# A graph-network layer with 203 instead of 191 of its 391 edge blocks summed by sorting on the chip

## The chip, the cores and the metric

One core of one Trainium2 chip runs the program. The metric is the time of one execution in microseconds on the device, the median over runs. Engines are named as in the profile: PE (TensorE matmul) with PEld (its weight loads), DVE (VectorE), ACT (ScalarE), POOL (GpSimd) and SP (SyncE, which here only issues DMAs).

## The reference

200,000 edges join 6,250 nodes, with 128 features a node. The edges come sorted by `dst`; `src` is random.

```python
h = jnp.maximum(_layernorm(x, axis=-1), 0.0)
x_ = h @ W_in
W_ij = shifted_softplus(f_ij @ W_f1 + b_f1) @ W_f2 + b_f2      # f_ij: 20 features an edge
W_ij = W_ij * f_ij_cutoff
x_ij = x_[dst] * W_ij                                           # one row of 128 an edge
out = jax.ops.segment_sum(x_ij, src, num_segments=6250)         # summed by source node
return x + shifted_softplus(out @ W_o1 + b_o1) @ W_o2 + b_o2
```

## The kernel before

**Items and quads.** The edges are cut into 1563 chunks of 128, and four chunks make a *quad* (512 edges); there are 391. The main loop runs over *items*, one for each quad, and is unrolled in full: item i carries the stages of several quads, each at its own distance. For every quad PE computes `z` (L374), ACT the softplus in two steps (L379, L384), PE the filter `W` (L567, eight float32 passes) and the gather of node rows `xg` by a one-hot matmul (L559), ACT the scaled copy `xc` (L572), and DVE the product of `W` and `xc` (L582). What differs is how the rows of a quad reach their source nodes.

**Scattered quads.** 200 of the 391 write their product into a tile `s` (six buffers). POOL then issues one indirect DMA with accumulation for each chunk (L644, four for a quad), which adds 128 rows of 128 floats into one of four accumulators in DRAM, `acc0` to `acc3`. The first 12 of these quads ("plain") are first cleaned of rows with the same node by a matmul (`pp`, L594); the other 188 ("listed", in windows of 16 quads) find such rows by the comparison `eql` (L427) and the counts `lcnt` (L437), and each window ends with one scatter more. Which accumulator a scatter uses follows from its number: `acc_of` goes round two up to K2_END, three up to K3_END, then four, and leaves out `acc0` for the last 64. `acc2` and `acc3` are zeroed by SP's DMAs at the items in Z2 and Z3, ten pieces of 320 KB each.

**Grouped quads.** The other 191 (quads 8, 10, 12 ... 388; `mpq`, from MP0, MPGAPS and MPEND in `sorted_quads`) never go to DRAM. DVE splits the product in three bf16 parts (`part_rem`, L746, twice a quad) and makes one-hot columns `pm` (L732, four). PE permutes the rows by node group (`pq`, L758, eight matmuls) and takes out those that find no slot (`po`, L781, four), ACT copies the results (`sg`, L766, four), SP regroups them by four DMAs (`mst`, L773). Eight such quads make a *round*, which has four *units*: in a unit PE multiplies the regrouped rows with one-hot rows `so` (made by DVE, L845) in 12 matmuls a quad of 32 rows each (`un`, L860), and DVE adds the four results into `accT` in SBUF (L871). Rows without a slot are summed once for two quads (`over_pe` to `over_int`) and go to DRAM in one scatter.

**Order.** It is written out by hand: `put` and `at` hang each step on an item and on a point in it (`L`, `D0`, `PE1`, `PE2`, `D2` and so on; table `AT`), and each engine runs its own instructions strictly in the order in which they were recorded, apart from what the weight loads do ahead. `unit_slots` places the units on items of grouped quads whose third last was not grouped.

**The end.** After scatter 843 no scatter goes to `acc0`. From item 372 on, `acc0` is read back group by group (`r0t`, L1171), transposed by PE (`rtp`, L1178) and added to `accT` (L1184), beside the last items. After the last scatter and the last unit the tail reads `acc1` to `acc3` (L1513) and computes the output layer.

Of the kernel before, what the change touches and what calls it, by code (L numbers as in the profile page):

```python
# [8 lines left out]
BF16 = mybir.dt.bfloat16  # L9
I32 = mybir.dt.int32  # L10
# [10 lines left out]
P = 128  # L21
# [5 lines left out]
OVC = 128  # L27
SLOTS = GRP * BCAP + OVC
MP0 = 8
MPGAPS = (2,)  # L30
MPEND = 1
RND = 8
RKQ = 8
ULAG = 7
# [21 lines left out]
LLAG = 12  # L56
LASTLAG = 5
LCAP = 7
LZERO = (9, 11, 13, 45)
PW = 387  # L60
MW = 388
PREP_GAP = 9
# [13 lines left out]
def tile_gnn(ctx: ExitStack, tc: tile.TileContext, x, fB, cT, srcT, srcr, srci, dstr, win_, wf1, wf2, bias, bo1c, wo1,  # L76
# [20 lines left out]
    GN = NP // GRP  # L97
    ZR = 10 if ACC_R % 10 == 0 else 1
    ZEARLY = 3
    K1_END, K2_END, K3_END = 0, 16, 170  # L100
    Z2, Z3 = [0, 1, 1, 2, 2, 3, 3, 4, 4, 5], range(18, 58, 4)
    mpq = sorted_quads(NQ)
    mpi = {q: n for n, q in enumerate(mpq)}
    rounds = unit_rounds(mpq)
    uslots = unit_slots(rounds)
    units = {i for us in uslots for i in us}
# [31 lines left out]
    wk = edge.enter_context(tc.tile_pool(name="wk", bufs=2))  # L138
# [669 lines left out]
        mp[q]["row"] = t  # L808

    def over_eq(q):  # L810
        eq = wk.tile([P, P], BF16, tag="oeq", name="oeq", bufs=1)
        nc.vector.tensor_scalar(eq, mp[q].pop("row")[:, :P], mp[q]["so"], None, op0=ALU.is_equal)
        mp[q]["eq"] = eq

# [104 lines left out]
    with tc.manual_schedule():  # L919
# [126 lines left out]
        def at(i, point, fn, *a):  # L1046
            hooks.setdefault((i, point), []).append((fn, a))

        def put(name, base, fn, *a, busy=()):
            d, point = AT[name]  # L1050
            i = max(clear(base + d, busy) if busy else base + d, 0)
            at(i, point, fn, *a)
            return i
# [66 lines left out]
        busy = units | {prep_start(g) + k for g in range(1, NG) for k in range(5)}  # L1120
# [85 lines left out]
        if spread:  # L1206
            k = clear(mid + 9, busy, 2)
# [3 lines left out]
            k = clear(NQ - 1, busy, 2)  # L1211
# [25 lines left out]
        for r in range(-(-len(mpq) // RKQ)):  # L1237
# [5 lines left out]
            k = put("rk_count", i, rank_count, r, busy=units)  # L1243
            k = max(k + 1, i + AT["rk_own"][0])
            at(k, AT["rk_own"][1], rank_own, r)
            k = clear(max(k, i + AT["rk_over"][0]), units)
            at(k, AT["rk_over"][1], rank_over, r)
            k = max(k + 1, i + AT["rk_slot"][0])
# [5 lines left out]
        for w in range(NW):  # L1254
            for g in range(wsize[w] // 4):
# [9 lines left out]
                k = put("l_dup", i, l_dup, w, g)  # L1265
# [12 lines left out]
            k = clear(i + AT["l_sum"][0], units)  # L1278
# [4 lines left out]
            k = put("l_int", k, over_int, ("L", w))  # L1283
            at(k, "S", over_scatter, ("L", w))
        if LE:
            for k in range(NACC):
                at(LZERO[k], "L", zero_list, k)
        for q in mpq:
            put("pm", q, perm_oh, q)
            put("rem1", q, part_rem, q, 1)  # L1290
            put("rem2", q, part_rem, q, 2)
            put("ext", q, part_ext, q)
            if q + 4 in units:
                for s in range(4):
                    at(q + 3, "PE2", permute, q, s)
                for s in range(4):
                    at(q + 3, "PE2", perm_out, q, s)
                for h in range(2):
                    at(q + 4, "L", regroup, q, h)
            else:  # L1300
                for s in range(4):
                    put(f"p{s}", q, permute, q, s)
                    put(f"o{s}", q, perm_out, q, s)
                for h in range(2):
                    put(f"rg{h}", q, regroup, q, h)
            if mpi[q] % 2 or q == mpq[-1]:
                k = mpq[mpi[q] + 1] if mpi[q] + 1 < len(mpq) else q + 2
                put("over_pe", k, over_pe, q)
                put("over_out", k, over_out, q)
                put("over_idx", q, over_idx, q)  # L1310
                put("over_dg", q, over_dg, q)
                k = put("over_row", q, over_row, q, busy=units)
                put("over_eq", k, over_eq, q)
                k = put("over_sum", q, over_sum, q, busy=units)
                put("over_copy", k, over_copy, q)
                put("over_ji", k, over_ji, q)
                k = put("over_int", k, over_int, q)
                at(k, "S", over_scatter, q)
        last = mpq[-1]
        for r, us in enumerate(uslots):  # L1320
            for s, k in enumerate(us):
                for h in range(3):
                    d, point = AT[f"so{h}"]
                    at(max(k + d, us[s - 1] if s else uslots[r - 1][3] if r else 0), point, unit_oh, r, s, h)
                put("unit", k, unit_pe, r, s)
                put("evac", k, unit_evac, r, s)

# [100 lines left out]
    with tc.For_i(0, redo, 1):  # L1428
# [8 lines left out]
        with tc.For_i(0, trips, 1) as ci:  # L1437
# [12 lines left out]
                cm, engines=[SP], min_val=0, max_val=EP // P - 1,  # L1450
                skip_runtime_bounds_check_because="a column of the table")
            nc.sync.dma_start(xcol, dropd[:, bass.ds(cr, 1)])
            sb = wk.tile([P, P], I32, bufs=1, tag="oeq", name="fsb")
            nc.sync.dma_start(sb, srcr.rearrange("s e -> (s e)")[bass.ds(ci * P, P)].unsqueeze(0).to_broadcast([P, P]))
            ft = wk.tile([P, P], BF16, tag="oh", name="fft")
            nc.vector.memset(ft[96:P, :], 1.0)
# [32 lines left out]
            eq = wk.tile([P, P], F32, tag="eq", name="feq", bufs=3)  # L1489
# [3 lines left out]
            s = wk.tile([P, P], F32, bufs=1, tag="dg", name="fs")  # L1493
# [118 lines left out]
def sorted_quads(nq):  # L1612
    qs, q = [], MP0
    while q < nq - MPEND:
        qs.append(q)
        q += MPGAPS[(len(qs) - 1) % len(MPGAPS)]
    return qs
# [10 lines left out]
def unit_slots(rounds):  # L1628
    end = rounds[-1][-1]
    grouped = {q for qs in rounds for q in qs}  # L1630
    out, used = [], set()
    for r, qs in enumerate(rounds):
        a = qs[-1] + ULAG
        last = r == len(rounds) - 1
        step = 2 if last else (rounds[r + 1][-1] - qs[-1]) / 4
        us = []
        for s in range(4):
            i = a + int(s * step)
            while i in used or (not last and i <= end and not UCLASSES[UCLASS](i, grouped)):
                i += 1  # L1640
            used.add(i)
            us.append(i)
        out.append(us)
    return out
# [10 lines left out]
def clear(i, busy, n=1):  # L1655
    while any(i + k in busy for k in range(n)):
        i += 1
    return i
# [11 lines left out]
def prep_start(g):  # L1670
    busy = unit_its(sorted_quads(4 * PREP_GAP * (g + 8)))
    return clear(7 + PREP_GAP * (g - 1), busy, 2) - 1
# [100 lines left out]
```

## Time and profile before

| | |
|---|---|
| median of 3 runs | 1912.47 us (1911.3 to 1914.54) |
| the profiled execution | 1918.46 us, of which the span of instructions 1916.7 us |
| mean granted TensorE clock | 0.96 |
| DMA engines' mean busy share | 0.8 in most slices of the span, 177 GB/s |
| scatters (L644) | 907: 751 of listed quads, 48 of plain ones, 108 of overflows and window sums |

The span divides into a start (to about 60 us), the loop over the items (to about 1825 us), the drain of the last grouped quads (to 1867 us) and the tail (to 1917 us). The profile's chain of what ended last reaches back only to 1867 us, and so covers the tail alone; what sets the pace of the loop must be read from the share of busy time of the engines in single stretches, and from who waits for whom.

### The profile page before, as it was taken

Reading aid. Unit: us, or ns where it says so; the run is one execution under the profiler, and the core shown is the slowest. Engines: PE = TensorE matmul, PEld = TensorE weight load, DVE = VectorE, ACT = ScalarE, POOL = GpSimd, SP = SyncE. Lnnn points to the kernel's source line nnn. Section 1 sums busy time; section 2 is a strip of 40 time slices with the busy share of each in tenths; the row PEclk is TensorE's granted clock in tenths of the full one; section 3 lists DMA queues with packets and bytes.
Section 4 is the critical chain, followed back from the end, with each engine's and each line's share of the span. In section 5 each row is a group of like instructions: output and inputs, shape, how many; then the busy total and the mean of one; then the engine's idle time right before and its main releaser. Section 6 shows DMA issues by size and latency. Waiting matters only on the chain. (4 is left out here: it accounts for less than half of the span.)

```text
span 1916.7 us, 55067 instructions
## 1 busy us (share of the span) xinstructions
PE 1676.3 (87%) x19124; PEld 1142.4 (60%) x19124; DVE 1600.0 (83%) x4692; ACT 1449.6 (76%) x4045; POOL 1509.3 (79%) x960
## 2 busy tenths in 40 slices
PE   4678898989998989989989989999999999978976
PEld 3555566656666666665656656666666566655644
DVE  5768897988898899899889888898897897976657
ACT  4668777867887888887878878887887888866615
POOL 5577768778888888888888888888888888887755
PEclk8789999999999999999999999999999999998988
DMA  8888888878888888888888888888888888868757
GB/s 294 229 197 198 191 186 173 175 153 160 172 180 168 162 177 172 162 188 162 164 175 180 168 171 178 174 179 174 173 183 155 172 183 170 169 121 185 130 116 267
DMA packets 366238, 339.58 MB, mean 177 GB/s; under 512 B 86685, under 2 KB 329292, under 8 KB 365956
## 3 DMA queue, kind: packets, MB, share of 16 engines
q1 hardware_dynamic: 233189, 269.78, 49.5%
q0 software_dynamic: 132208, 66.05, 33.0%
q8 instruction: 151, 2.47, 0.5%
q14 instruction: 132, 1.07, 0.2%
q10 hardware_dynamic: 558, 0.20, 0.0%
HBM read 151.16 MB, written 108.80 MB: 136 GB/s over the span
## 5 line engine op out<-in xcount | busy, mean ns | idle before, releaser
L644 POOL DMA_INDIRECT acc<-s,lji x751 | 1210.0, 1611 | 269.4 <-issue 177.0
L572 ACT ACTIVATE xc<-xg,cb 128x128 f32<-128x128 f32 x1564 | 447.5, 374 | 179.7 <-PE z L374 92.5
L567 PEld LDWEIGHTS W<-w,a 128*128 128x128 f32 x3128 | 430.0, 199 | 64.2 <-issue 50.9
L860 PE MATMUL un<-so,mst 32*128 32x392 bf16 x9168 | 425.1, 329 | 18.1 <-ACT sg L766 7.9
L567 PE MATMUL W<-w,a 128*128 128x128 f32 x3128 | 430.7, 282 | 0.8 <-issue 0.5
L766 ACT CAST sg<-pq 128x388 bf16<-128x388 f32 x764 | 342.1, 497 | 75.0 <-DMA mst<-sg 48.5
L758 PE MATMUL pq<-pt,pm 128*128 128x388 bf16 x1528 | 328.5, 337 | 30.5 <-ACT os L825 9.6
L860 PEld LDWEIGHTS <-mst 32*128 32x128 bf16 x9168 | 251.5, 94 | 166.8 <-issue 37.6
L384 ACT ACTIVATE a<-a,con 128x512 f32<-128x512 f32 x391 | 282.8, 723 | 11.6
L746 DVE TENSOR_TENSOR pt<-pt 128x512 f32<-128x512 f32 x382 | 259.6, 680 | 0.0
L871 DVE TENSOR_TENSOR accT<-un,accT 128x392 f32<-128x392 f32 x368 | 182.1, 556 | 80.0 <-PE z L374 26.6
L379 ACT ACTIVATE a<-z 128x512 f32<-128x512 f32 x391 | 243.7, 623 | 6.3 <-PE z L374 6.3
L758 PEld LDWEIGHTS <-pm 128*128 128x128 bf16 x1528 | 143.6, 98 | 145.4 <-issue 56.9
L845 DVE TENSOR_SCALAR so<-iot,mst 128x392 bf16<-128x392 f16 x764 | 215.6, 333 | 4.3 <-PE un L860 2.9
L374 PE MATMUL z<-ft,ws 123*128 123x512 bf16 x391 | 154.8, 397 | 63.9 <-DVE s L582 13.2
L582 DVE TENSOR_TENSOR s<-W,xc 128x512 f32<-128x512 f32 x188 | 128.8, 685 | 93.8 <-ACT xc L572 56.5
L644 POOL DMA_INDIRECT acc<-os,oji x108 | 173.6, 1607 | 40.9 <-issue 18.3
L732 DVE TENSOR_SCALAR pm<-iotp,pos 128x384 bf16<-128x384 f16 x764 | 201.3, 323 | 0.0
L582 DVE TENSOR_TENSOR pt<-W,xc 128x512 f32<-128x512 f32 x191 | 130.4, 683 | 49.2 <-ACT xc L572 23.9
L559 PE MATMUL xg<-wn,oh 63*128 63x128 bf16 x1564 | 158.0, 222 | 12.1 <-DVE oh L391 7.3
L556 PE MATMUL W<-b2rep,onesb 64*128 64x512 bf16 x391 | 155.1, 397 | 0.0
L781 PE MATMUL po<-pt,pm 128*128 128x387 bf16 x764 | 153.1, 343 | 1.3 <-DVE pt L746 1.1
(214 smaller groups left out, 1840.9 us busy)
## 6 DMA issues: line engine op xcount, KB each, us to landing
mst<-sg SPq DMA_DIRECT2D x764, 97.0 KB
sb<-src SPq DMA_DIRECT2D x100, 256.0 KB
rb<-reld SPq DMA_DIRECT2D x194, 128.0 KB
fsd<-f SPq DMA_DIRECT2D x49, 480.0 KB
ft<-fsd SPq DMA_DIRECT2D x96, 240.0 KB
fb<-in_fB_dram SPq DMA_DIRECT2D x49, 320.0 KB
ft<-fsd SPq DMA_DIRECT2D x96, 160.0 KB
acc<-s,lji POOLq DMA_INDIRECT x751
```

The source lines that it names most:

```text
L379: nc.scalar.activation(a, st[q]["z"], AF.Exp)
L384: nc.scalar.activation(a, a, AF.Ln, bias=half, scale=0.5)
L567: nc.tensor.matmul(W[:, c, :], st[q]["a"][:, c * P:(c + 1) * P], w2, start=False, stop=(c == 3))
L572: nc.scalar.mul(xc[:, c, :], st[q]["xg"][:, c, :], late["c", q // CQ][:, 4 * (q % CQ) + c:4 * (q % CQ) + c + 1])
L582: nc.vector.tensor_tensor(m[:, :, :P], st[q]["W"], st[q]["xc"], op=ALU.mult)
L644: nc.gpsimd.indirect_dma_start(out=accs[k][:rows, :], out_offset=bass.IndirectOffsetOnAxis(ap=ji, axis=0), in_=s, in_offset=None, compute_ ...
L732: nc.vector.tensor_scalar(pm[:, c], iotp, rk[r]["pos"][:, 4 * j + c:4 * j + c + 1], None, op0=ALU.is_equal)
L746: nc.vector.tensor_tensor(pt[:, :, k * P:(k + 1) * P], a, high(a), op=ALU.subtract)
L758: nc.tensor.matmul(t[:, :MW], mp[q]["pm"][:, c, s * P:(s + 1) * P], high(mp[q]["pt"][:, c:c + 1, :MW])[:, 0], start=(c == 2 * h), stop=(c ...
L766: nc.scalar.copy(mp[q]["sg", h][:, s], mp[q].pop(("q", k))[:, :MW])
L845: nc.vector.tensor_scalar(so, iotw[:, :GN], w[:, 3 * P // 2:3 * P // 2 + 1], None, op0=ALU.is_equal)
L860: nc.tensor.matmul(ts[g][:, :GN], mp[q]["ms", s // 2][v, s % 2, k * P:(k + 1) * P], mp[q]["oh"][v], start=(q == qs[0] and k == 0), stop=(q ...
```

## The change

203 quads are grouped: the gaps between grouped quads are now 2, 2, 2, 2, 1, 2, 2, 2 in turn, so that in each run of eight two stand in neighbouring items (16 and 17, 31 and 32, 46 and 47 ...), and eight grouped quads take 15 items instead of 16. That makes 26 rounds (the last of three quads) instead of 24 (the last of seven). 188 quads are left to scatter, 16 of them plain and 172 listed, in 11 windows instead of 12. Scatters become 864: 751 - 64 + 1 of listed quads, 64 of plain ones, 113 of the rest.

For the first quad of a neighbouring pair the later copies and the second regroup move to points further on in its item; overflow rows get a second buffer for `oeq`; `so` of a unit may stand at the point `D2`; and `over_sum` is placed after `over_eq`. `acc2` is used from scatter 12 (16 before) and `acc3` from scatter 100 (170 before), and their zeroing is moved: `acc3`'s ten pieces to items 14, 17 ... 41 (18, 22 ... 54 before).

```diff
-MPGAPS = (2,)
-MPEND = 1
+MPGAPS = (2,2,2,2,1,2,2,2)
+MPEND = 2
...
-LZERO = (9, 11, 13, 45)
+LZERO = (9, 11, 13, 41)
...
-    K1_END, K2_END, K3_END = 0, 16, 170
-    Z2, Z3 = [0, 1, 1, 2, 2, 3, 3, 4, 4, 5], range(18, 58, 4)
+    K1_END, K2_END, K3_END = 0, 12, 100
+    Z2, Z3 = [0, 1, 1, 2, 2, 3, 3, 3, 3, 3], range(14, 44, 3)
...
-        eq = wk.tile([P, P], BF16, tag="oeq", name="oeq", bufs=1)
+        eq = wk.tile([P, P], BF16, tag="oeq", name="oeq", bufs=2)
...
                 for s in range(4):
                     put(f"p{s}", q, permute, q, s)
-                    put(f"o{s}", q, perm_out, q, s)
+                    if q + 1 in mpi and s > 1:
+                        at(q + 4, "PE1", perm_out, q, s)
+                    else:
+                        put(f"o{s}", q, perm_out, q, s)
                 for h in range(2):
-                    put(f"rg{h}", q, regroup, q, h)
+                    if q + 1 in mpi and h:
+                        at(q + 4, "PE2", regroup, q, h)
+                    else:
+                        put(f"rg{h}", q, regroup, q, h)
             if mpi[q] % 2 or q == mpq[-1]:
-                k = mpq[mpi[q] + 1] if mpi[q] + 1 < len(mpq) else q + 2
+                k = mpq[mpi[q] + 1] if mpi[q] + 1 < len(mpq) else q + 3
...
-                k = put("over_sum", q, over_sum, q, busy=units)
+                k = put("over_sum", max(q, k + 1 - AT["over_sum"][0]), over_sum, q, busy=units)
...
-                    at(max(k + d, us[s - 1] if s else uslots[r - 1][3] if r else 0), point, unit_oh, r, s, h)
+                    b = us[s - 1] if s else uslots[r - 1][3] if r else 0
+                    at(max(k + d, b), "D2" if k + d <= b else point, unit_oh, r, s, h)
```

How the order moves is seen best on DVE. Before, from the product of grouped quad 242 (`pt<-W`) to that of the scattered quad 243 behind it (`s<-W`):

```order
L582 TENSOR_TENSOR pt<-W,xc 128x4x128
L324 TENSOR_REDUCE fmax<-fb 128x1
L732 TENSOR_SCALAR pm<-iotp,pos 128x384 x4
L699 TENSOR_REDUCE rank<-rkp 128x32
L702 TENSOR_SCALAR ov<-rank 128x32
L444 TENSOR_SCALAR ldup<-lcnt,con 128x16
L391 TENSOR_SCALAR oh<-rb,con 128x512
L746 TENSOR_TENSOR pt<-pt 128x4x128
L582 TENSOR_TENSOR s<-W,xc 128x4x128
```

Now, on the same engine, from the product of grouped quad 241 to that of its neighbour 242, which is grouped too:

```order
L582 TENSOR_TENSOR pt<-W,xc 128x4x128
L655 TENSOR_SCALAR srcf<-srcT_sb 128x32
L658 TENSOR_SCALAR cnt<-srcf 128x32
L659 TENSOR_SCALAR cnt<-cnt 128x32
L662 TENSOR_TENSOR G<-iot,cnt 128x512
L732 TENSOR_SCALAR pm<-iotp,pos 128x384 x4
L845 TENSOR_SCALAR so<-iot,mst 128x392 x2
L525 TENSOR_SCALAR leq<-orow,idl 128x128
L812 TENSOR_SCALAR oeq<-orow,ovs 128x128
L427 TENSOR_TENSOR eql<-sb,srcT_sb 128x1024
L746 TENSOR_TENSOR pt<-pt 128x4x128
L582 TENSOR_TENSOR pt<-W,xc 128x4x128
```

No scattered product stands between the two, so each of the two items carries one-hot columns and a split.

The second place is POOL, at its scatters 101 to 105, counted from 0. Before, they go round three accumulators:

```order
L644 DMA acc2_77<-os_3397,oji_3561 6400x128
L644 DMA acc0_75<-s_3567,lji_1379 7936x128
L644 DMA acc1_76<-s_3567,lji_1379 7936x128
L644 DMA acc2_77<-s_3567,lji_1379 7936x128
L644 DMA acc0_75<-s_3567,lji_1379 7936x128
```

Now, at scatters 102 to 106, they go round four:

```order
L644 DMA acc2_77<-os_3716,oji_3871 6400x128
L644 DMA acc3_78<-s_3877,lji_1376 7808x128
L644 DMA acc0_75<-s_3877,lji_1376 7808x128
L644 DMA acc1_76<-s_3877,lji_1376 7808x128
L644 DMA acc2_77<-s_3877,lji_1376 7808x128
```

`acc3` has come in, so that four scatters instead of three lie between two that add to the same accumulator.

More of the change, by code (lines that the diff above doesn't have):

```diff
@@ L1452, in tile_gnn @@
             nc.sync.dma_start(xcol, dropd[:, bass.ds(cr, 1)])
-            sb = wk.tile([P, P], I32, bufs=1, tag="oeq", name="fsb")
+            sb = wk.tile([P, P], I32, bufs=2, tag="oeq", name="fsb")
             nc.sync.dma_start(sb, srcr.rearrange("s e -> (s e)")[bass.ds(ci * P, P)].unsqueeze(0).to_broadcast([P, P]))
```

## The prediction

> **What bounds the kernel now.** I read the page's busy shares first, then the same shares in two long stretches of the loop, then the scatters against the products that feed them, and last who waits for whom.
>
> The page offers three candidates, and the windows put them beside the number of items: the second answer counts the `z` matmuls, one for each item. The first stretch still holds the preparation of the node rows (layer norm, `W_in`), the second doesn't.
>
> ```profile
> PE 1676.3 (87%) x19124; PEld 1142.4 (60%) x19124; DVE 1600.0 (83%) x4692; ACT 1449.6 (76%) x4045; POOL 1509.3 (79%) x960
> ...
> core 0: us, PE busy (x) PEld busy (x) DVE busy (x) ACT busy (x) POOL busy (x), PEclk, DMA share, GB/s
> 450.00:1050.00 600.00, 546.17 (x6438) 369.94 (x6440) 534.35 (x1623) 484.72 (x1375) 498.98 (x309) 0.98 0.84 171
> 1130.00:1690.00 560.00, 518.57 (x6237) 351.39 (x6237) 490.58 (x1436) 459.56 (x1282) 467.98 (x291) 1.00 0.85 173
> ...
> 450.00:1050.00 600.00, 51.12 (x131) 12.49 (x130) 0.98 0.84 171
> 1130.00:1690.00 560.00, 50.04 (x130) 12.36 (x129) 1.00 0.85 173
> 1690.00:1800.00 110.00, 7.58 (x19) 1.83 (x19) 0.91 0.78 154
> ```
>
> An item takes 600/131 = 4.58 us in the first and 560/130 = 4.31 us in the second. PE is busy 91.0% and 92.6%, DVE 89.1% and 87.6%. POOL seems idle for 17% and is not: it did 309 and 291 scatters, one each 1.94 and 1.92 us, and the row of L644 below gives 1.61 us for one, with 177 us of idle "issue" over 751, that is 0.24 (0.30 before most of them in the timeline). 1.61 + 0.30 = 1.91 us: POOL goes from scatter to scatter without a real pause. So either POOL sets the pace or it only just keeps up. The backlog tells: scatters done (first answer) against products done (second).
>
> ```profile
> 0.00:400.00 400.00, 258.65 (x160) 0.92 0.86 203
> 0.00:1000.00 1000.00, 756.49 (x468) 0.95 0.84 183
> 0.00:1690.00 1690.00, 1332.98 (x825) 0.97 0.85 179
> ...
> 0.00:400.00 400.00, 52.00 (x76) 0.92 0.86 203
> 0.00:1000.00 1000.00, 140.87 (x206) 0.95 0.84 183
> 0.00:1690.00 1690.00, 249.56 (x365) 0.97 0.85 179
> ```
>
> Of the first 76, 206 and 365 quads 42, 107 and 186 are scattered ones (all but 8, 10, 12 ...): 168, 428 and 744 scatters due, with some 15, 52 and 96 for overflows and windows (one for two grouped quads, one a window). So about 23, 12 and 15 scatters wait for POOL. Six `s` buffers hold 24. Near 400 us the buffers are nearly full and POOL can hold DVE up; at 1000 and 1690 us they are half empty. POOL neither starves there nor blocks. What blocks is shown by the waits: for a scatter to free a buffer, DVE waited only this often, and all of it before 420 us.
>
> ```profile
> DVE s L582 <- DMA acc<-s,lji: 8.4, 4, 3.1
> PE rtp L1178 <- DMA r0t<-acc: 11.6, 1, 11.6
> SPq L1171 <- DMA acc<-os,oji: 16.3, 1, 16.3
> ACT sg L766 <- DMA mst<-sg: 48.5, 21, 12.9
> ```
>
> So from 400 us on the loop goes at the pace of PE and DVE, which feed each other; POOL runs level with it. The one place where POOL's backlog costs is the second row: SP's first read of `acc0` waits 16.3 us for its last scatters to land, and PE, in order, 11.6 us for that read.
>
> **The change, part by part.** The costs come from these groups.
>
> ```profile
> L860 PE MATMUL un<-so,mst 32*128 32x392 bf16 x9168 | 425.1, 329 | 18.1 <-ACT sg L766 7.9 <-issue 3.9 <-DVE so L845 1.5
> L758 PE MATMUL pq<-pt,pm 128*128 128x388 bf16 x1528 | 328.5, 337 | 30.5 <-ACT os L825 9.6 <-issue 4.2 <-ACT s L602 3.1
> L781 PE MATMUL po<-pt,pm 128*128 128x387 bf16 x764 | 153.1, 343 | 1.3 <-DVE pt L746 1.1 <-DVE accT L871 0.2
> L594 PE MATMUL pp<-m,eq 128*128 128x129 f32 x96 | 18.1, 353 | 8.9 <-DVE m L582 4.8 <-DVE jd L614 4.1
> L437 PE MATMUL lcnt<-wgtb,eql 128*128 128x1 bf16 x752 | 26.1, 163 | 14.3 <-DVE eql L427 7.1 <-ACT sg L766 5.8 <-DVE accT L871 0.7
> L845 DVE TENSOR_SCALAR so<-iot,mst 128x392 bf16<-128x392 f16 x764 | 215.6, 333 | 4.3 <-PE un L860 2.9 <-issue 0.8 <-DMA mst<-sg 0.6
> L732 DVE TENSOR_SCALAR pm<-iotp,pos 128x384 bf16<-128x384 f16 x764 | 201.3, 323 | 0.0
> L746 DVE TENSOR_TENSOR pt<-pt 128x512 f32<-128x512 f32 x382 | 259.6, 680 | 0.0
> L871 DVE TENSOR_TENSOR accT<-un,accT 128x392 f32<-128x392 f32 x368 | 182.1, 556 | 80.0 <-PE z L374 26.6 <-PE un L860 18.6 <-PE xg L559 16.0
> L427 DVE TENSOR_TENSOR eql<-sb,srcT_sb 128x1024 bf16<-128x1024 int16 x94 | 63.7, 678 | 6.8 <-DMA sb<-src 6.8
> L766 ACT CAST sg<-pq 128x388 bf16<-128x388 f32 x764 | 342.1, 497 | 75.0 <-DMA mst<-sg 48.5 <-issue 11.7 <-PE pq L758 10.6
> L644 POOL DMA_INDIRECT acc<-s,lji x751 | 1210.0, 1611 | 269.4 <-issue 177.0 <-DMA acc<-s,lji 43.2 <-DVE pt L746 6.9
> ```
>
> I take the busy time of a group by its count, since matmuls overlap.
>
> PE: 576 more `un` at 425.1/9168 = 46 ns, +26.7 us; 96 `pq` at 215 ns, +20.6; 48 `po` at 200 ns, +9.6; four more plain quads at 18.1/12 us, +6.0; 64 `lcnt` fewer at 35 ns, -2.2. Sum +61 us.
>
> DVE: 48 `so` at 282 ns, +13.5; 48 `pm` at 264 ns, +12.7; 24 splits at 680 ns, +16.3; 32 additions to `accT` (two more rounds of 16) at 495 ns, +15.8; 8 `eql` fewer at 678 ns, -5.4. Sum +53 us. Products are as many as before. Ranks, overflows and one window fewer leave a few us either way, which I set to nothing.
>
> ACT: 48 `sg` at 448 ns, +21.5 us, on an engine that is busy 81%: covered, unless PE waits for these copies; that would be seen at L758 and L374.
>
> POOL: 43 scatters fewer at 1.91 us, -82 us. SP: 48 more `mst` issues, with 6 loads and 4 window reads fewer; SP waits mostly for others, so nothing.
>
> The question is what +61 us on PE and +53 us on DVE make of the loop. The two stretches above are an experiment of the kernel itself: preparation adds to each item (546.17/131 - 518.57/130) = 0.18 us on PE, 0.305 on DVE, 0.165 on ACT, and the item gets 0.27 us longer, 0.89 us for each us on DVE. By DVE the change costs 0.89 x 53 = 47 us. By PE, at its unchanged share of 92%, 61/0.92 = 66 us. Were half of PE's idle share in the two stretches (95 of 1160 us) filled up, 1600 us of loop would hide 66 us, and the cost would be about 0. I take 53, near DVE's value, as that is the nearer experiment; bounds 0 and 66.
>
> Of POOL's 82 us I credit only what others waited for. First, the stall at `acc0`: with a backlog of next to nothing, the read comes at once. That gives 11.6 us, and some more, as the clock in the 110 us around it was granted at 0.91: 15 (bounds 0 and 20; only 19 items fell in these 110 us). Second, the early waits for `s` buffers, 8.4 us; with four accumulators from scatter 100 POOL is also faster there: 8 (bounds 0 and 20). Third, the drain (the last line is from the chain of waits, the tail's first read):
>
> ```profile
> 1823.19 1.16 PE L567 MATMUL W<-w,a 128*128 128x128 f32 x8
> 1863.71 1.98 DVE L871 TENSOR_TENSOR accT<-un,accT 128x392 f32<-128x392 f32 x4 [3.27 <-PE un L860]
> 1867.00 0.38 SPq L1513
> ```
>
> From the last `W` to the last unit pass 42 us, four units of seven quads (84 `un` each, 3.9 us) and their additions in turn. The last round now has three quads (1.7 us), but one unit more of the round before stands behind the last item: 4 x 2.2 - 4.5 = 4 us.
>
> Second buffer of `oeq`, placing of `so` and `over_sum`: no gain claimed, DVE hardly waits there. `acc3`'s zeroing in 28 items instead of 37: ten DMAs of 320 KB closer together, at 0.84 to 0.86 DMA share, could hold up `mst` (the 48.5 us of ACT's waits): 0, at most 10.
>
> Sum: 53 - 15 - 8 - 4 = +26 us on the profiled execution's 1918.5, so 1944.5. The median of the runs lies 6.0 us under the profiled time: 1938.
>
> **A rule weighed.** The trace gives PE's weight loads as busy 369.94 of 600 us, 62%, where its matmuls have 91%. The Trainium skill (Perfetto Trace Analysis, Identifying the Most-Contended Engine) says that matmul busy time doesn't tell how near PE is to its limit, and that the share of weight loads does. By that rule PE has a third of its time to spare and hides all of its 61 us, and the sum would be 0 - 27, or 1885 in the median, against 1938 by the preparation's row and 1951 by PE's own share. The trace agrees in part only: records of `un` overlap, but PE's idle time is no larger than 8%.
>
> **The rivals.**
>
> *PE has room, and POOL's relief shows (faster).* The added matmuls fill gaps, since 8% of PE's time is idle in front of DVE and ACT. For it: the overlapped records of `un` (329 ns each, 46 ns apart). Against it: the preparation's 0.18 us on PE did lengthen the item. If two thirds of the bound of 66 were hidden, the loop would cost 22, the credits 27 to 45: 1918.5 - 14 to -23, or about 1890 to 1899 in the median. The rule above speaks for this rival. If POOL set the pace throughout, 82 us would go, to 1830; the half empty buffers speak against it, 4 in 100.
>
> *A pair overloads DVE (slower still).* In the two items of a pair DVE has columns and a split in each, and a unit two items away. If every pair cost a further 1.5 us that nothing makes up, with 25 pairs and PE's bound: 66 + 37 - 27 = +76, 1988. It decides from the point where DVE's idle share, 11 to 12%, can't take up a pair's 2 us by the next unit; I think it can.
>
> *Nothing measurable.* Cost and credits both near 27: within 0.2% (4 us, about what a measurement can tell).
>
> **How the numbers follow.** Likeliest, slower at 1916.5 to 1962 (cost 30 to 66, credits 16 to 35): 51 in 100, with 1938 at its middle. Slower still, over 1962: 9. Same, 1908.5 to 1916.5: 10. Faster: 30, of which 22 between 1886 and 1908.5, 8 below. Slower together 60. The range 1886 to 1962 leaves out 8 below and 9 above.
>
> **What would show it.** Right: an item between 1130 and 1690 us takes longer (about 4.45 instead of 4.31 us); POOL has gaps that end with DVE's products; the wait of PE for `r0t` is gone; DVE's busy share rises above 90%. Wrong: items of 4.3 us or less with PE above 95%, which would mean that the gaps were room; or POOL still back to back. A wait of POOL for zeroing near scatter 100, or of ACT for `mst`, would add to the time.

## The result, and the profile after

The changed kernel took 2092.47 us (median of 4 runs, 2086.54 to 2106.23) against 1911.88 us for the kernel before: a ratio of 1.0946, 95% interval 1.0894 to 1.0998. That is 154 us above the forecast of 1938 us and 130 us above the upper end of its range. The sign was right and the size was not. The profiled execution took 2086.54 us, its span 2084.8 us. Its profile has the 864 scatters of the plan: 687 of listed quads (751 - 64), 64 of plain ones and 113 of the rest.

The first view is the page's row of busy shares. Then come the two stretches of the loop, first all engines, then the `z` matmuls, which count the items.

```profile
PE 1768.9 (85%) x19842; PEld 1195.5 (57%) x19842; DVE 1658.6 (80%) x4858; ACT 1483.2 (71%) x4140; POOL 1438.1 (69%) x917
```

```profile
450.00:1050.00 600.00, 532.61 (x6121) 356.69 (x6121) 506.74 (x1541) 452.42 (x1282) 417.70 (x258) 0.96 0.74 154
1130.00:1690.00 560.00, 497.61 (x5855) 333.58 (x5854) 452.46 (x1302) 420.57 (x1172) 401.86 (x251) 0.97 0.76 156
...
450.00:1050.00 600.00, 47.16 (x119) 11.44 (x120) 0.96 0.74 154
1130.00:1690.00 560.00, 45.46 (x115) 11.04 (x115) 0.97 0.76 156
```

The busy times moved the way that was forecast (whole page: PE +93, DVE +59, ACT +34, POOL -71 us; PE's is 32 us above the sum, at a mean granted clock of 0.948 instead of 0.960), but every share fell. An item takes 600/119 = 5.04 us instead of 4.58 in the first stretch, and 560/115 = 4.87 instead of 4.31 in the second, where 4.45 had been forecast. PE is busy 89% where it had been 91 to 93%, DVE 81 to 84% instead of 88 to 89%. More work with lower shares on all engines points to a new wait. The view of who waits for whom shows it:

```profile
POOL acc L644 <- DVE s L582: 149.7, 59, 6.0
DVE s L582 <- ACT xc L572: 128.3, 64, 9.2
ACT sg L766 <- DMA mst<-sg: 96.2, 34, 8.6
PE un L860 <- ACT sg L766: 38.0, 13, 7.1
PE z L374 <- DMA ft<-fsd: 22.6, 2, 19.9
```

The second and the last of these rows before (the third, 48.5 us, and the 7.9 us of the fourth stand in the prediction's lines):

```profile
DVE s L582 <- ACT xc L572: 56.5, 46, 4.3
PE z L374 <- DMA ft<-fsd: 10.1, 2, 8.9
```

Read from the third row: ACT stands before the copy of permuted rows into `sg`, waiting for the regroup DMA that still reads the tile; this was 48.5 us in 21 waits. The fourth row shows what stands behind it: PE waits for those copies with a unit behind them, 38 us instead of 7.9. The second: DVE's product waits for ACT's `xc`, which stands behind the same copies in ACT's order, up to 9.2 us at a time. The first: POOL, level with the loop before, now waits 150 us for products.

Here is the longest item of the steady loop in the timeline, behind the pair of quads 196 and 197 (start, length, engine, line, idle time before it and what ended it):

```profile
1045.49 0.85 ACT L766 CAST sg<-pq 128x388 bf16<-128x388 f32 x2
1046.40 0.42 SPq L337 DMA_DIRECT2D fsd<-f  x1
1047.24 0.90 ACT L766 CAST sg<-pq 128x388 bf16<-128x388 f32 x2
1048.65 1.35 SPq L358 DMA_DIRECT2D rb<-reld  x2
1048.70 0.87 ACT L766 CAST sg<-pq 128x388 bf16<-128x388 f32 x2
1051.06 1.75 SPq L367 DMA_DIRECT2D wn<-tab  x4
...
1053.81 1.15 SPq L773 DMA_DIRECT2D mst<-sg  x2
1055.17 0.42 SPq L309 DMA_DIRECT2D tab<-x  x1
1055.63 4.47 SPq L773 DMA_DIRECT2D mst<-sg  x6
1058.11 0.87 ACT L766 CAST sg<-pq 128x388 bf16<-128x388 f32 x2 [8.54 <-DMA mst<-sg]
1058.64 6.26 PE L860 MATMUL un<-so,mst 32*128 32x392 bf16 x94 [7.09 <-ACT sg L766]
1061.29 0.69 DVE L582 TENSOR_TENSOR s<-W,xc 128x512 f32<-128x512 f32 x1 [9.19 <-ACT xc L572]
```

ACT fills an `sg` tile with two copies, and a quad needs two tiles, so a pair needs four. There are three. By 1049.6 us three are full, the first of them since 1046.3. The DMAs that would empty it are SP's to issue, and SP, in its order, first issues a store and other loads until 1053.8; the two issues take 1.2 us, and by 1058.1 the tile is free. ACT waits 8.5 us, and in the same stretch PE stands for 7.1 us with 94 matmuls of a unit behind, and DVE for 9.2 us. This is the pattern of most of this wait: counted in the order of the copies, 17 of ACT's 34 waits and 56 of the 96 us stand before the fourth tile of one of the 25 pairs.

### The profile page after: what moved, and what is told of

The parts are those of the page before. It is cut to its first block, busy times and chain, and to the rows that moved or that the text cites. A ratio compares the mean times of both kernels' runs of the same rounds, so it can differ in the third digit from the quotient of the medians.

```text
span 2084.8 us, 56776 instructions
## 1 busy us (share of the span) xinstructions
PE 1768.9 (85%) x19842; PEld 1195.5 (57%) x19842; DVE 1658.6 (80%) x4858; ACT 1483.2 (71%) x4140; POOL 1438.1 (69%) x917
## 5 line engine op out<-in xcount | busy, mean ns | idle before, releaser
L644 POOL DMA_INDIRECT acc<-s,lji x687 | 1107.6, 1612 | 369.8 <-issue 164.1
L860 PE MATMUL un<-so,mst 32*128 32x392 bf16 x9744 | 483.9, 337 | 61.8 <-ACT sg L766 38.0
L766 ACT CAST sg<-pq 128x388 bf16<-128x388 f32 x812 | 363.8, 494 | 156.9 <-DMA mst<-sg 96.2
L860 PEld LDWEIGHTS <-mst 32*128 32x128 bf16 x9744 | 287.1, 96 | 233.1 <-issue 99.9
L758 PE MATMUL pq<-pt,pm 128*128 128x388 bf16 x1624 | 361.0, 341 | 42.4 <-ACT s L602 7.1
L746 DVE TENSOR_TENSOR pt<-pt 128x512 f32<-128x512 f32 x406 | 276.6, 681 | 0.0
L871 DVE TENSOR_TENSOR accT<-un,accT 128x392 f32<-128x392 f32 x400 | 198.4, 557 | 88.9 <-PE xg L559 32.6
L582 DVE TENSOR_TENSOR s<-W,xc 128x512 f32<-128x512 f32 x172 | 118.3, 688 | 155.1 <-ACT xc L572 128.3
L845 DVE TENSOR_SCALAR so<-iot,mst 128x392 bf16<-128x392 f16 x812 | 226.8, 332 | 5.3 <-PE un L860 5.2
L732 DVE TENSOR_SCALAR pm<-iotp,pos 128x384 bf16<-128x384 f16 x812 | 215.5, 326 | 0.0
```

Source lines behind the costliest of these rows:

```text
L582: nc.vector.tensor_tensor(m[:, :, :P], st[q]["W"], st[q]["xc"], op=ALU.mult)
L644: nc.gpsimd.indirect_dma_start(out=accs[k][:rows, :], out_offset=bass.IndirectOffsetOnAxis(ap=ji, axis=0), in_=s, in_offset=None, compute_ ...
L732: nc.vector.tensor_scalar(pm[:, c], iotp, rk[r]["pos"][:, 4 * j + c:4 * j + c + 1], None, op0=ALU.is_equal)
L746: nc.vector.tensor_tensor(pt[:, :, k * P:(k + 1) * P], a, high(a), op=ALU.subtract)
L758: nc.tensor.matmul(t[:, :MW], mp[q]["pm"][:, c, s * P:(s + 1) * P], high(mp[q]["pt"][:, c:c + 1, :MW])[:, 0], start=(c == 2 * h), stop=(c ...
L766: nc.scalar.copy(mp[q]["sg", h][:, s], mp[q].pop(("q", k))[:, :MW])
```

## The experiments

The runs were made in five batches on four chips, with the kernel before timed beside every version; it took 1911.8 to 1915.7 us in each. Ratios are to it. The chips are called A (first batch), B (second), C (third and fourth) and D (fifth). The versions with pairs turned out to differ by some 40 us between chips, so times of theirs are safely compared on one chip alone. Which chip gave the result above isn't known.

**A fourth `sg` tile, a moved unit, no pairs.** The first three versions and the fourth, which joins the first two, went in one batch, on chip A. The theory is that three buffers for four tiles are the cause. The other versions ask what the unit four items behind a pair has to do with it, and what the change does without pairs.

```diff
-            mp[q]["sg", h] = wk.tile([P, 2, MW], BF16, tag="eq", name="sg", bufs=3)
+            mp[q]["sg", h] = wk.tile([P, 2, MW], BF16, tag="eq", name="sg", bufs=4)
...
-        s = sp_.tile([P, 132], F32, tag="os", name="os", bufs=6)
+        s = sp_.tile([P, 132], F32, tag="os", name="os", bufs=5)
```

(`eq` and `feq` share the buffers of `sg` and go to four with it; `os` makes the room.)

> The changed kernel with a fourth buffer for sg (and five for os instead of six, to make the room). Theory A (buffers): in a pair the four sg tiles of two quads are filled within one item, there are three, and ACT stands until a regroup DMA has landed; then ACT's wait for DMA mst<-sg falls from 96 us to under 40, the item before the late unit and the unit's own fall from 6.4 and 8.5 us to about 5 and 6, and the time to 1960 to 2010 us. Theory B (place of the unit): what costs is that all eight permutations and four copies of the pair's second quad are put into the one item before the unit, on top of the first quad's second half; PE and ACT are then late whatever the buffers; the time stays above 2050 us. Theory C (SP's order or DVE's load near the pair): 2070 to 2100 us.

Measured: 1958.85 us (1958.09 to 1964.17), ratio 1.0234 (1.0204 to 1.0264), just under the range of theory A. ACT's wait for regroup DMAs fell to 7.6 us.

```diff
-UCLASSES = (lambda i, g: i in g and i - 3 not in g, lambda i, g: i in g, ...
+UCLASSES = (lambda i, g: i in g and i - 3 not in g and not (i - 4 in g and i - 5 in g), lambda i, g: i in g, ...
```

> The changed kernel with one more condition on where a unit may stand: not four items after the second quad of a pair, so that this quad's permutations and copies are spread over two items as elsewhere. Theory B: the late item of 8.5 us goes, time 1950 to 2010 us, and ACT's wait for DMA mst<-sg falls too, with the three buffers left. Theory A: sg is still short in the pair, ACT's wait stays near 90 us and the time above 2040 us. Theory C: no change beyond 1 per cent.

Measured: 2023.55 us, 1.0577 (1.0541 to 1.0612), between the ranges of A and B. With the unit out of the way PE waited only 4.7 us for `sg` copies, and ACT still 47.3 us for the regroup DMAs:

```profile
ACT sg L766 <- DMA mst<-sg: 47.3, 24, 7.4
PE un L860 <- ACT sg L766: 4.7, 6, 2.6
```

```diff
-MPGAPS = (2,2,2,2,1,2,2,2)
+MPGAPS = (2,)
```

> The changed kernel with the old gap of 2 throughout: 191 grouped quads, no pair; the accumulators, the zeroing, the second oeq buffer and the placing of so and over_sum as in the changed kernel. All three theories: the pairs carry the loss, so 1895 to 1920 us; the prediction gave the earlier accumulators 8 us of gain at most. Above 1950 us the loss would lie in the accumulators, the zeroing or the moved steps.

Measured: 1903.91 us, 0.9955 (0.9934 to 0.9976). All the rest of the change, with 191 quads grouped as before, is slightly faster than before.

> Both: the unit moved off the pair and a fourth sg buffer. If A and B are each a part: 1930 to 1960 us, the time that the prediction gave the added work alone (1938). If B is all, no better than the moved unit alone (within 0.5 per cent); if A is all, no better than the fourth buffer alone.

Measured, fourth tile and moved unit together: 1984.45 us, 1.0375 (1.0341 to 1.0408). With four tiles the move harms by 26 us, as theory A has it: the unit's place by itself was not the fault. With three tiles it does matter, since the unit stands behind the wait in PE's order: with the unit moved away the fourth tile is worth only 2023.6 - 1984.5 = 39 us, against the 92 to 95 us found below with the unit in its place. The changed kernel itself was not timed on chip A, so what the move alone gains there isn't known; against chip D's 2056 us, where the four-tile version takes the same time as on A, it would be some 33 us, an estimate.

**SP freed, half the pairs, and the stall at `acc0`.** The next four, on chip B, ask what makes the tile late, whether the loss goes with the number of pairs, and what the credit of 15 us was worth.

```diff
-        wn = ld.tile([P, 2, P], BF16, tag="wn", name="wn")
+        wn = ld.tile([P, 2, P], BF16, tag="wn", name="wn", bufs=4)
...
-        s = sp_.tile([P, 132], F32, tag="os", name="os", bufs=6)
+        s = sp_.tile([P, 132], F32, tag="os", name="os", bufs=5)
```

> The changed kernel, three sg buffers, with a fourth buffer for the node rows wn (five os instead of six): SP no longer has to wait for PE before it may load wn (L367 waited 82 + 35 us), with the regroup DMAs behind it in its queue. If the sg tiles are held too long because SP issues their regroup late, ACT's wait for DMA mst<-sg falls well below 96 us and the time to 2000 to 2060 us. If three tiles are too few in a pair however early SP is, the wait stays above 80 us and the time within 1 per cent of 2092 us.

Measured: 2075.79 us, 1.0841 (1.0798 to 1.0885). ACT's wait for regroup DMAs went from 96.2 to 88.9 us.

```diff
-        nc.sync.dma_start(fsd[b].rearrange("g (p e) -> p g e", p=P), f3)
+        if b > 1:
+            at(fst_at[b] + 2, "A1", fb_store, b)     # the same store, two items later
+        else:
+            fb_store(b)
```

> The changed kernel, three sg buffers, with the store of the split edge features (L337 before, on which SP waits 81 us for DVE) issued two items later, when its data have long been there. If SP's lateness holds the sg tiles: 2030 to 2075 us and a smaller wait of ACT for mst. If the number of tiles alone counts: within 1 per cent of 2092 us.

Measured: 2075.38 us, 1.0842 (1.08 to 1.0884), with 76.9 us of that wait. Each takes away one of SP's waits, and each comes out about 17 us under the 2092 of the changed kernel, which wasn't timed on this chip, so that the gain isn't shown beyond doubt. (Both profiles have the late starts of the last section, as the changed kernel's has, which speaks for chips of one kind.) The first meets its second forecast, three tiles too few however early SP is: the time stayed within 1 per cent and the wait above 80 us. The second freed SP only in part: its 81 us of waiting for DVE in front of the store turned into 61 us in front of the loads that read the store back. So SP's order probably adds to the lateness, and neither load alone makes it.

```diff
-MPGAPS = (2,2,2,2,1,2,2,2)
+MPGAPS = (2,2,2,2,1,2,2,2,2,2,2,2,2,2,2,2)
```

> The changed kernel with one pair in sixteen grouped quads instead of eight: 197 grouped, half as many pairs, three sg buffers. If the loss goes by the number of pairs, half way between no pair (1904) and the change (2092): 1985 to 2010 us. If a pair only hurts where the added work on PE and DVE has filled the item anyway, less than half: below 1970 us.

Measured: 2013.18 us, 1.0519 (1.0473 to 1.0565), just above the range of a loss by the number of pairs. Half the pairs cost 109 of the 189 us between the kernel without pairs and the changed one, though the three were not timed on one chip. Some 20 of the 109 fell in the first ten items, which took 94 us here, 72 without pairs and 80 with all pairs.

```diff
-MPGAPS = (2,2,2,2,1,2,2,2)
+MPGAPS = (2,)
...
-    RET = max(120, sum(scat) - 64)
+    RET = max(120, sum(scat) - 88)
...
-            i = clear(max(r0_at + 1, ret_at + 5), units)
+            i = clear(max(r0_at + 1, ret_at + 15), units)
```

> The version without pairs, with acc0 given up 24 scatters earlier (88 before the end instead of 64) while its read back stays at the same items. If the stall of PE in front of that read (20.7 us there, 11.6 us in the kernel before) lies on the path, it goes and 1904 becomes 1882 to 1892 us; if the work only moves on to POOL's end, no change.

Measured: 1902.16 us, 0.993 (0.9907 to 0.9954): some 2 us less than without this edit (5 by the ratios, which allow for the two chips) instead of 12 to 22. PE's wait for the read of `acc0` (20.7 us in the version without it) is gone, and the `z` of the last item comes 20 us sooner; but from there to the last addition the drain takes 65.6 instead of 49.8 us. In its timeline the reason is SP's reads for the last window sum, and a unit that stands in PE's order behind that sum:

```profile
1806.35 26.12 SPq L513 DMA_DIRECT2D lm<-acc  x4
...
1830.46 0.80 PE L531 MATMUL lsum<-lm,leq 128*128 128x128 f32 x2 [14.01 <-DMA lm<-acc]
...
1835.09 6.61 PE L860 MATMUL un<-so,mst 32*128 32x392 bf16 x84
```

A stall taken away in one place had covered another.

**The same tile where there are no pairs.** The next four were made on chip C. If three tiles were simply too few, a fourth would help the kernel before as well, where ACT waited 48.5 us.

```diff
 (the kernel before, or the version of the last diff)
-  tag="eq", name="sg", bufs=3     ->  +  bufs=4
-  tag="os", name="os", bufs=6     ->  +  bufs=5
-  tag="s", name="s", bufs=6       ->  +  bufs=5
```

> The kernel before, with four sg tiles instead of three; to make room s goes from six buffers to five and os from six to five. Theory (the fourth sg tile is worth 134 us to the changed kernel because two neighbouring quads need four tiles at a time): without pairs a fourth tile is worth little. ACT waited 48.5 us for regroup DMAs in the kernel before, but PE waited only 7.9 us for such copies, so 0 to 15 us are gained, less what one s buffer fewer costs (DVE waited 8.4 us for s with six): 1895 to 1920 us. Rival (three tiles are too few at any density, and the 134 us would have been had without the change): about half of it or more is gained here too, 1850 us or less.

Measured: 1914.01 us, 1.0021 (1.0002 to 1.004). The view of the tile `sg` lists all that ACT waits for in front of these copies (us, times):

```profile
  PE pq L758: 14.7, 35
  issue: 6.6, 26
  DMA rb<-reld: 1.0, 3
  DMA fb<-in_fB_dram: 0.2, 1
```

The 48.5 us for regroup DMAs are gone entirely, and the time is what it was. DVE, with one `s` buffer fewer, waited 13.9 us for scatters instead of 8.4; so little can hide there.

> The version without pairs and with the earlier read of acc0 (1902 us with three sg tiles), now with four sg tiles, s and os five each. Theory: ACT's 39 us of waits for regroup DMAs go, little of which others waited for: 1885 to 1903 us. Rival (three tiles too few at any density): 1850 us or less.

Measured: 1905.75 us, 0.9971 (0.9951 to 0.9991), against 1902.16 with three tiles on chip B: nothing gained there either.

In the changed kernel, a fifth tile (`s` and `os` five each):

> The changed kernel with five sg tiles (s and os five each). Theory (four tiles are enough for a pair; what remains is the added work of PE and DVE): with four tiles ACT waited only 7.6 us for regroup DMAs, so at most 8 us more are gained: 1945 to 1970 us. Rival (regrouping still holds the items behind a pair): 1930 us or less.

Measured: 2006.57 us, 1.0481 (1.0442 to 1.0521). ACT's wait for regroup DMAs was down to 1.5 us, yet this was 48 us more than with four tiles on chip A, and above both forecasts. That left open what the fourth had been worth.

And the accumulators alone, in the kernel before:

```diff
-    K1_END, K2_END, K3_END = 0, 16, 170
-    Z2, Z3 = [0, 1, 1, 2, 2, 3, 3, 4, 4, 5], range(18, 58, 4)
+    K1_END, K2_END, K3_END = 0, 12, 100
+    Z2, Z3 = [0, 1, 1, 2, 2, 3, 3, 3, 3, 3], range(14, 44, 3)
```

> The kernel before with the change's accumulator numbers alone (acc2 from scatter 12, acc3 from scatter 100, zeroing of acc3 at items 14 to 41), all quads grouped and scattered as before. Theory (POOL is level with the loop and waits for s only early): DVE's 8.4 us of early waits and some of POOL's 43.2 us of waits for the accumulators go: 1898 to 1913 us. Rival (ten DMAs of 320 KB closer together hold up the regroup DMAs and loads): 1915 to 1930 us, with more than 48.5 us of ACT's waits for mst.

Measured: 1901.58 us, 0.9956 (0.9935 to 0.9978), and ACT's wait for regroup DMAs 40.5 us: no harm of the closer zeroing shows, and the earlier accumulators give 8 us (4 to 12 by the interval). DVE's early waits for `s` fell from 8.4 to 1.7 us.

**Was it the tile or the chip?** Four more versions on chip C, then the changed kernel and its four-tile version beside each other on chip D.

> The changed kernel with four sg tiles, s six and os five, as in the first experiment, once more beside the other versions. If its 1959 us hold: 1955 to 1968 us. If that run was a chance: near 2007 us, as with five sg and five s tiles.

Measured, the program of the first experiment again: 2000.74 us, 1.0455 (1.0408 to 1.0503), against 1958.85 us on chip A.

> The changed kernel with four sg tiles, but s from six buffers to five. Theory (a scattered product needs its s tile while POOL still works off the four scatters of each of the five before; a pair's POOL gap is followed by products in a row): the s tile missing costs the 48 us, 2000 to 2010 us, and a fifth sg tile is worth nothing. Rival (it was the fifth sg tile that cost, by letting ACT's copies run ahead of what PE needs next): 1955 to 1968 us here. In both, ACT's waits for regroup DMAs stay under 15 us.

Measured, four `sg` and five `s` tiles: 1997.76 us, 1.0439 (1.0398 to 1.048).

> The changed kernel with three sg tiles and s from six buffers to five. If an s tile is worth 48 us by itself: 2130 to 2145 us. If three sg tiles hide what s costs, because both hold the same items behind a pair: 2085 to 2105 us, as before this edit.

Measured, three `sg` and five `s` tiles: 2090.12 us, 1.091 (1.0869 to 1.0951). So on chip C the fourth tile is worth 2090 - 1998 = 92 us, an `s` tile nothing, and a fifth `sg` tile nothing. Both theories of the expectation for four and five tiles fell, though the first had the time right: it was neither `s` nor the fifth tile, but the chip. In its two batches chip C gave 2007, 2001 and 1998 us for versions with four or five `sg` tiles.

> Half as many pairs (197 quads grouped, one pair in sixteen) with four sg, five s and five os tiles. With three sg tiles the half took 109 us of the 189 us that all pairs take. If what remains with four sg tiles grows with the added work of PE and DVE (half of 55 us): 1925 to 1945 us. If the s tile is what misses with pairs, some 20 us more: 1945 to 1965 us.

Measured, half the pairs with four tiles: 1943.36 us, 1.0151 (1.011 to 1.0192). The time lies in the first range by luck: that took half of chip A's 55 us, and on chip C all pairs with four tiles cost 1998 - 1906 = 92 us, of which this is 38.

> The changed kernel unchanged, beside the version with four sg tiles on the same chip. Theory (the fourth tile is worth about 90 us on any chip, and the first experiment's chip ran every version with pairs some 40 us faster): near 2092 us with the four-tile version near 2000 us, or near 2050 us with that near 1959 us; in both cases the difference is 80 to 100 us. Rival (the fourth tile is worth 134 us and the later runs of it were held up by something else): a difference of 125 us or more.

Measured: 2056.08 us (2049.12 to 2058.6), 1.0723 (1.0699 to 1.0747).

> The changed kernel with four sg, five os and six s tiles, a third time, beside the changed kernel itself. Theory: 80 to 100 us less than that in the same call, and where the time is near 2000 us the additions to accT show waits that end with z, xg and W of PE as in the second run (43 us); where it is near 1959 us they end with un alone. Rival: 125 us less or more.

Measured: 1961.51 us (1952.22 to 1967.71), 1.0234 (1.0205 to 1.0262). The fourth tile is worth 2056 - 1962 = 95 us here, much as on chip C, and the kernel is 34 to 39 us faster than there with either number of tiles. The rows on ACT's and PE's waits, first the changed kernel, then four tiles (no row for PE, since it no longer waited for these copies):

```profile
ACT sg L766 <- DMA mst<-sg: 101.8, 36, 8.5
PE un L860 <- ACT sg L766: 48.0, 20, 7.0
```

```profile
ACT sg L766 <- DMA mst<-sg: 10.7, 4, 7.3
```

And the four-tile version's stretches on chip D, to be read beside those of the changed kernel above:

```profile
450.00:1050.00 600.00, 541.08 (x6471) 366.16 (x6470) 530.69 (x1616) 475.38 (x1343) 444.46 (x274) 0.98 0.79 165
1130.00:1690.00 560.00, 514.28 (x6233) 347.33 (x6236) 486.91 (x1415) 454.34 (x1265) 428.00 (x267) 0.98 0.81 167
...
450.00:1050.00 600.00, 49.52 (x125) 12.01 (x125) 0.98 0.79 165
1130.00:1690.00 560.00, 48.69 (x124) 11.80 (x123) 0.98 0.81 167
```

PE is back at 90 and 92%, DVE at 88 and 87%, and an item takes 4.80 and 4.52 us: 0.2 us more than before the change, where the forecast had 0.14. On chip C the same program takes 4.88 and 4.59 us.

| pairs | three `sg` tiles | four | worth of the fourth |
|---|---|---|---|
| none | 1912 (C), 1902 us (B) | 1914, 1906 us (C) | nothing |
| one in sixteen quads grouped (half) | 2013 (B) | 1943 (C) | 70 us (two chips) |
| one in eight (the change) | 2090 (C); 2056 (D) | 1998 (C); 1962 (D) | 92; 95 us |

Undoing only the later copies and regroups of a pair's first quad wasn't tried; so how much of the shortage comes from their place, and how much from the pair itself, isn't shown.

## Why the prediction was wrong, point by point

**The step that failed** is ACT's line in the part on the change: "+21.5 us, on an engine that is busy 81%: covered, unless PE waits for these copies", and with it SP's "48 more `mst` issues ... so nothing". Both charged the copies and the issues for their length alone; the "unless" named the wait and gave it no price. What a pair adds is not length but tiles in use at once: four, with three to be had and the fourth released by a DMA that SP issues late. Of the 154 us that the forecast missed, 92 to 95 are this wait, shown by taking it away on two chips and by the tile's being worth nothing without pairs. ACT's waits for regroup DMAs stood in the prediction, 48.5 us, and were charged at most 10, as a matter of the zeroing. Their length says little: the 48.5 us of before cost nothing, and the 91 us that the fourth tile took away on chip D cost 95. That this is because a unit of PE and the product's `xc` now stand behind them is read from the waits; the moved unit bears it out, since with it the tile's worth fell to 39 us. The Trainium skill (Perfetto Trace Analysis, Optimization Strategy) says that the same gap repeating on the engine that should be saturated can mean too few buffers for the next tile. The trace agrees: the gaps of PE before `un` that end with `sg` are 13 of up to 7.1 us.

**The added work was priced well for one kind of chip and too low for another.** From the version without pairs to the one with pairs and a fourth tile it cost 1903.91 to 1958.85 us on chip A: +55, forecast 53 between 0 and 66. In the middle of the loop (items 90 to 368) the spans differ by 72 us, over the upper bound, and later items and the drain give some back. On chip C the nearest step is 1905.75 to 1997.76 us: +92, outside the bounds. (The first of these two also has the earlier read of `acc0`, worth 2 to 5 us, which the second lacks.) The rival that PE's gaps would hide it is out: with no tile to wait for, PE's share came back to where it was and the item got longer. The Trainium skill (Perfetto Trace Analysis, Identifying the Most-Contended Engine) judges PE's headroom not by matmul busy time but by, among other things, the share of its weight loads; from this the prediction made a rival with PE's 61 us hidden. With four tiles the weight loads were 61 and 62% busy, and the item still got longer; but these runs don't part PE's added work from DVE's, which came with it, and so don't decide that rule.

**The credits were too high.** 27 us were forecast; everything but the pairs, together, gave 9 us on chip A. The early waits for `s`: 8 forecast, 8 measured with the accumulators alone. The stall at `acc0`: 15 forecast; it did vanish, as the waits show, but where it was removed by itself it gave only 2 to 5 us, since another wait in the drain took its place. The drain: 4 forecast, nothing seen; from the last item's `z` to the end pass 102 us instead of 100, the last addition comes 5 us sooner, but the tail's first read does not.

**The start** had no term. The first ten items took 80 us instead of 72; PE waits 22.6 us there for `ft`, 10.1 before. It goes with the pairs' version and not with the accumulators (72 without pairs); its cause stays open.

**The sum, done again.** Chip A's terms, -9 for the rest of the change and +55 for pairs with a fourth tile, give 1916 - 9 + 55 = 1962 on chip D, where 1962 was measured; with the 95 us of the missing tile 2057, measured 2056. On chip C the steps are 1912 - 8 + 92 + 92 = 2088, measured 2090. The result, 2092, fits chip C, and its profile has that chip's late starts (last section). Against the forecast that is 92 us for the tile, some 39 for added work above the 53, and some 18 for credits that didn't come, as far as these two can be parted: about 149 of the 154. Why the pairs with a fourth tile cost 37 us more on one chip than on another stays open.

**Signs that were named.** The item longer than 4.31, POOL's gaps ending with products, PE's wait for `r0t` gone: all seen. DVE above 90%: not, its share fell; that was the sign of a wait. "A wait ... of ACT for `mst` would add to the time": it did. The rival of a pair that overloads DVE was nearest, with 1988 us, but named the wrong engine and counted 1.5 us a pair where the fourth tile shows 92/25 = 3.7. In the rival that PE has room one sum is off: a cost of 22 less credits of 27 to 45 gives -5 to -23, so 1890 to 1908 instead of 1890 to 1899.

## What to carry to other kernels

When a change moves two users of a small ring of tiles next to each other, count how many tiles are in use at once, and follow who releases them: here a tile was full at 1046.3 us, and the DMA that frees it came up in SP's order at 1053.8. Price a wait by what stands behind the waiting instruction in its engine's order, not by its length: in this kernel 48 us of the same wait cost nothing before the change and 91 us of it cost 95 after it. More work with lower busy shares on every engine was the mark of a new wait here; look for one before the work is blamed. And compare versions on one chip: the same program differed by 40 us between two of them.

## What the runs showed of the hardware

The same program (four `sg` tiles) took 1958.85 us on chip A, 1961.51 on D and 2000.74 on C, with runs close together on each, while the kernel before took 1914, 1916 and 1913 us there. The profiles differ in one respect that we found. These are DVE's waits ahead of its additions to `accT`, on chip C and then on chip D:

```profile
  PE un L860: 31.6, 27
  PE z L374: 24.2, 16
  PE xg L559: 18.0, 15
  issue: 4.7, 5
  PE W L567: 0.4, 1
```

```profile
  PE un L860: 43.8, 55
  issue: 2.3, 3
```

On chip D the addition starts some 30 ns after the end of the unit's last matmul in the records, in nearly every case in which it waited. On chip C 33 of the 64 additions that waited start more than 0.3 us after it, up to 1.6 us, many of them at the end of matmuls that they don't need, and the waits sum to 79 instead of 46 us. The profiles fall in two kinds by this sign: those of chips A and D start on time, those of chips B and C, of the changed kernel in the result and of the kernel before start late. The versions without pairs differ in the same way, on time on A and late on B and C, with hardly a difference in time (1904, 1902 and 1906 us). So why only the versions with pairs pay for it stays open, and that the late starts are the cause of the 40 us isn't shown.
